# Two pipelined halves in one fixed order per step: attention over time, then attention over bands with feed-forward in the same step

## The chip, the cores and the metric

The kernel runs on one core of one Trainium2 chip. The metric is the device time of one execution in microseconds; most executions agree within 0.3%. The TensorE clock is granted by a throttle; the profile gives it as a share of full speed.

TensorE does the matmuls (PE in the profile, its weight loads PEld), VectorE is DVE, ScalarE is ACT, GpSimd is POOL. SBUF is working memory, PSUM the accumulator that matmuls write.

## The reference

One block of a model on x of shape 2 x 256 x 128 x 128 (batch, time T, bands F, channels C), all in fp32: three residual branches, each with a layer norm.

```python
xt = _ln(x, ln_t_w, ln_t_b).transpose(0, 2, 1, 3)
x = x + _mha(xt, ..., H_T, causal_mask).transpose(0, 2, 1, 3)   # attention over T, 4 heads of 32
xf = _ln(x, ln_f_w, ln_f_b)
x = x + _mha(xf, ..., H_F, band_mask)                           # attention over F, |i - j| <= 16
xn = _ln(x, ln_n_w, ln_n_b)
h = gelu(xn @ w1.T + b1)                                        # 128 -> 512
x = x + (h @ w2.T + b2)                                         # 512 -> 128
```

## The kernel before

Work is cut into groups of 512 rows (NT = 4 tiles of 128). The first half has 128 groups of attention over time and writes x1 to DRAM. The second half loads 16 time steps at a time, does band attention for four groups and then feed-forward for the same four. Program order is group after group; a scheduler may reorder each engine's queue.

```python
def attention_bands(self, src, dst, after):
    qT, kT, v = self.project(src, 1)          # norm, transpose xp -> xnT, qp, kp, vp
    sp = self.ps_s.tile([P, H, 512], F32, name="sp")
    ...                                       # 16 score matmuls
    p = self.pw.tile([P, H, NT * P], F32, name="pb", tag="p")
    for h in range(0, H, 2):
        e = nc.scalar.activation(p[:, h : h + 2], sp[:, h : h + 2], AF.Exp)
        ...                                   # two masks on POOL
    op = self.ps.tile([P, NT * P], F32, name="op", tag="ps")   # values
    sm = self.ps.tile([P, NT * P], F32, name="sm", tag="ps")   # row sums, by a matmul with ones
    ...
    self.add_attended(dst, op, sm, 1)         # divide on DVE, yp = oT @ wo, add

def feed_forward(self, cur, res, after):
    xnT = self.norm_transposed(lambda i: cur[:, i, :])
    for j in range(NI):
        hp = ps.tile([P, NT * P], F32, name="hp", tag="ps")    # one bank each, four rotate
        nc.tensor.matmul(hp, self.w1[:, j * P : (j + 1) * P], xnT, start=True, stop=True)
        e = nc.scalar.activation(hT[:, j, :], hp, AF.Gelu, bias=..., scale=1.0)
    zp = ps.tile([P, NT, P], F32, name="zp", tag="ps")
    ...

# PSUM, eight banks: four for the scores, four that rotate for everything else
self.ps_s = ctx.enter_context(tc.tile_pool(name="ps_s", bufs=1, space=PSUM))
self.ps = ctx.enter_context(tc.tile_pool(name="ps", bufs=4, space=PSUM))
```

## Time and profile before

| | before |
|---|---|
| time | 5907.1 us, median of 3 |
| TensorE busy / mean clock | 69% / 0.81 |
| first half | 128 groups of 17.2 us |
| second half | 128 groups of 28.7 us |
| PE busy and clock, 100 to 2200 us | 67%, 0.83 |
| PE busy and clock, 2300 to 5800 us | 72%, 0.79 |

The busy row counts an engine from start to end of its instructions. A TensorE busy share below 100% at a clock below 1 has two losses in it: time without a matmul, and matmuls that run at half rate. The prediction shows the lines.

### The profile page before, as it was taken

Reading aid. Unit: us, or ns where it says so; the run is one execution under the profiler, and the core shown is the slowest. Engines: PE = TensorE matmul, PEld = TensorE weight load, DVE = VectorE, ACT = ScalarE, POOL = GpSimd, SP = SyncE. Lnnn points to the kernel's source line nnn. Section 1 sums busy time; section 2 is a strip of 40 time slices with the busy share of each in tenths; the row PEclk is TensorE's granted clock in tenths of the full one; section 3 lists DMA queues with packets and bytes.
Section 4 is the critical chain, followed back from the end, with each engine's and each line's share of the span. In section 5 each row is a group of like instructions: output and inputs, shape, how many; then the busy total and the mean of one; then the engine's idle time right before and its main releaser. Section 6 shows DMA issues by size and latency. Waiting matters only on the chain. (4 is left out here: it accounts for less than half of the span.)

```text
span 5915.1 us, 79997 instructions
## 1 busy us (share of the span) xinstructions
PE 4105.8 (69%) x33318; PEld 2701.9 (46%) x33318; DVE 2042.5 (35%) x6314; ACT 1603.7 (27%) x1984; POOL 1805.4 (31%) x2086
## 2 busy tenths in 40 slices
PE   5666666666666666767677766767776776777677
PEld 3444444444444444445444444544444454444445
DVE  4333333333333323333333333333333333333332
ACT  2222222222222222223222222222222232222222
POOL 3222223222222222333333333333323333332332
PEclk9888888888888788778777887877787787788778
DMA  2111111111111110000000000000000000000000
GB/s 56 31 31 29 38 31 30 31 31 29 38 31 29 29 29 26 15 15 22 22 15 17 27 15 15 24 20 15 17 27 15 15 26 18 15 17 27 8 8 16
DMA packets 222867, 140.70 MB, mean 24 GB/s; under 512 B 7968, under 2 KB 205984, under 8 KB 222496
## 3 DMA queue, kind: packets, MB, share of 16 engines
q1 hardware_dynamic: 221248, 134.45, 8.2%
q8 instruction: 264, 4.33, 0.3%
q10 hardware_dynamic: 1248, 1.05, 0.1%
q14 instruction: 107, 0.88, 0.0%
HBM read 68.36 MB, written 67.11 MB: 23 GB/s over the span
## 5 line engine op out<-in xcount | busy, mean ns | idle before, releaser
L193 DVE TRANSPOSE_TENSOR_REDUCE st<-sm 128x16 f32<-128x512 f32 x256 | 183.3, 716 | 2402.1 <-PE sm L306 1473.5
L163 ACT COPY xnT<-xp 128x512 f32<-128x512 f32 x384 | 224.7, 585 | 2570.5 <-PE xp L161 2570.5
L294 POOL TENSOR_SCALAR_AFFINE_SELECT pb<-pb 128x1024 f32<-128x1024 f32 x512 | 541.0, 1091 | 1154.0 <-ACT pb L290 1154.0
L304 PE MATMUL op<-pb,v 128*32 128x128 f32 x4096 | 372.6, 409 | 611.7 <-POOL pb L294 611.7
L304 PEld LDWEIGHTS op<-pb,v 128*32 128x32 f32 x4096 | 216.4, 156 | 759.3 <-POOL pb L294 707.1
L216 PE MATMUL hp<-xnT,w1T_sb 128*128 128x512 f32 x1024 | 521.0, 651 | 39.0 <-ACT xnT L163 23.4
L224 PEld LDWEIGHTS zp<-w2T_sb,hT 128*128 128x128 f32 x4096 | 487.5, 192 | 61.5 <-issue 59.6
L224 PE MATMUL zp<-w2T_sb,hT 128*128 128x128 f32 x4096 | 499.0, 275 | 0.1
L153 POOL TENSOR_SCALAR rstd<-mv 128x4 f32<-128x4 f32 x384 | 92.0, 242 | 1311.3 <-DVE mv L151 1311.3
L217 ACT ACTIVATE hT<-hp,bias 128x512 f32<-128x512 f32 x512 | 351.9, 687 | 458.9 <-PE hp L216 458.4
L205 PE MATMUL yp<-f_woT_sb,oT 128*128 128x128 f32 x1024 | 234.2, 402 | 330.4 <-DVE oT L202 330.4
L252 POOL TENSOR_SCALAR_AFFINE_SELECT p<-p 128x512 f32<-128x512 f32 x512 | 313.2, 634 | 487.3 <-ACT p L249 487.2
L364 POOL TENSOR_TENSOR res<-x,rows_sb 128x512 f32<-128x512 f32 x128 | 162.1, 1266 | 976.6 <-DVE x L206 842.0
L205 PE MATMUL yp<-t_woT_sb,oT 128*128 128x128 f32 x1024 | 205.8, 363 | 341.4 <-DVE oT L202 341.4
L306 PE MATMUL sm<-pb,ones 128*32 128x512 f32 x1024 | 442.4, 962 | 0.0
L205 PEld LDWEIGHTS yp<-f_woT_sb,oT 128*128 128x128 f32 x1024 | 196.5, 286 | 512.9 <-DVE oT L202 512.9
L249 ACT ACTIVATE p<-sp 128x1536 f32<-128x1536 f32 x256 | 371.2, 1450 | 210.8 <-PE sp L245 200.2
L178 ACT ACTIVATE kT<-kp,bias 128x512 f32<-128x512 f32 x256 | 175.9, 687 | 868.4 <-PE kp L176 868.4
L154 POOL TENSOR_TENSOR rstd<-rstd,mhalf 128x4 f32<-128x4 f32 x384 | 403.5, 1053 | 16.2
L158 DVE TENSOR_SCALAR xh<-xb,mv,rstd 128x128 f32<-128x128 f32 x512 | 273.0, 596 | 326.0 <-PE xp L161 234.9
L205 PEld LDWEIGHTS yp<-t_woT_sb,oT 128*128 128x128 f32 x1024 | 172.8, 255 | 375.9 <-DVE oT L202 375.9
L270 PE MATMUL op<-p,v 128*32 128x256 f32 (+1 forms) x4096 | 281.9, 376 | 89.1 <-POOL p L252 89.1
(99 smaller groups left out, 6390.0 us busy)
## 6 DMA issues: line engine op xcount, KB each, us to landing
xt<-in_x SPq DMA_DIRECT2D x64, 512.0 KB, 5.4
x<-rd SPq DMA_DIRECT2D x256, 128.0 KB, 1.9
out<-res SPq DMA_DIRECT2D x128, 256.0 KB, 2.3
xb<-x SPq DMA_DIRECT2D x32, 0.5 KB, 6.2
w1T_sb<-in_w1T ACTq DMA_DIRECT2D x1, 256.0 KB, 4.1
w2T_sb<-in_w2T ACTq DMA_DIRECT2D x1, 256.0 KB, 4.5
t_wiT_sb<-in_t_wiT ACTq DMA_DIRECT2D x1, 192.0 KB, 2.6
f_wiT_sb<-in_f_wiT ACTq DMA_DIRECT2D x1, 192.0 KB, 4.0
```

What stands on the lines that cost most here:

```text
L154: nc.gpsimd.tensor_tensor(rstd, rstd, self.mhalf, ALU.pow)
L158: nc.vector.tensor_scalar(xh[:, i, :], src(i), mv[:, i, 0:1], rstd[:, i : i + 1], ALU.subtract, ALU.mult)
L205: nc.tensor.matmul(yp[:, i], oT[:, i * P : (i + 1) * P], self.wo[a], start=True, stop=True)
L216: nc.tensor.matmul(hp, self.w1[:, j * P : (j + 1) * P], xnT, start=True, stop=True)
L217: e = nc.scalar.activation(hT[:, j, :], hp, AF.Gelu, bias=self.bias[:, 4 + j : 5 + j], scale=1.0)
L224: nc.tensor.matmul(zp[:, i], hT[:, j, i * P : (i + 1) * P], self.w2[:, j, :], start=(j == 0), stop=(j == NI - 1),)
L249: e = nc.scalar.activation(p, sp[:, :, 0 : 3 * P], AF.Exp)
L252: nc.gpsimd.affine_select(out=d, in_=d, compare_op=ALU.is_ge, fill=0.0, base=0, pattern=[[0, H], [1, P]], channel_multiplier=-1,)
L270: nc.tensor.matmul(to[r, t0 + (2 - m) * P : t0 + 2 * P], v[:, 2 * s + n // 2, r] if left is None else left, p[:, h, n * P : (n + m) * P], ...
L294: nc.gpsimd.affine_select(out=d, in_=d, compare_op=ALU.is_ge, fill=0.0, base=BAND, pattern=[[0, 2 * NT], [s, P]], channel_multiplier=-s,)
L304: nc.tensor.matmul(op[r, t], v[:, i, r], p[:, h, t], start=True, stop=True)
L306: nc.tensor.matmul(sm[h * D : (h + 1) * D], self.ones, p[:, h], start=True, stop=True)
```

## The change

The intent is to keep TensorE fed. Each group's work is cut into phases; a loop issues, in every step, phases of neighbouring groups in one order on TensorE, DVE, ACT and POOL, and the scheduler may not change it. Band attention and feed-forward (two groups behind) share a step. PSUM is split anew: four banks for scores **or** hidden (one buffer), one each for op and sm, two that rotate for xp, qp, kp, vp, yp and zp.

```diff
+    def hidden(self, g):
+        nc, NI = self.nc, self.NI
+        hp = self.ps_s.tile([P, NI, 512], F32, name="hp", tag="s")
+        g.hT = self.work.tile([P, NI, NT * P], F32, name="hT", bufs=2)
+        for j in range(NI):
+            nc.tensor.matmul(
+                hp[:, j], self.w1[:, j * P : (j + 1) * P], g.xnT, start=True, stop=True
+            )
+            nc.scalar.activation(
+                g.hT[:, j], hp[:, j], AF.Gelu, bias=self.bias[:, 4 + j : 5 + j], scale=1.0
+            )
...
+    def pipeline(n, phases):
+        ...
+        for t in range(-before, n + behind):
+            for f, off in phases:
+                if 0 <= t + off < n:
+                    f(t + off)
...
-        self.ps = ctx.enter_context(tc.tile_pool(name="ps", bufs=4, space=PSUM))
+        self.ps_o = ctx.enter_context(tc.tile_pool(name="ps_o", bufs=1, space=PSUM))
+        self.ps = ctx.enter_context(tc.tile_pool(name="ps", bufs=2, space=PSUM))
+        ET = mybir.EngineType
+        ctx.enter_context(
+            tc.manual_schedule(engines={ET.PE, ET.DVE, ET.Activation, ET.Pool})
+        )
...                                            # first half: 14 phases; second half:
+        self.pipeline(len(hs), [
+            (load_b, 8),
+            (add_y_b, -1),
+            (lambda n: self.scores_bands(hs[n]), 0),
+            (lambda n: self.norm_turn(hs[n]), -2),          # xp, xnT of feed-forward
+            (lambda n: self.project_q(hs[n], 1), 1),
+            (lambda n: self.norm_apply(hs[n], lambda i: hs[n].x[:, i, :]), 2),
+            (lambda n: self.project_kv(hs[n], 1), 1),
+            (stats_b, 3),
+            (lambda n: self.hidden(hs[n]), -2),
+            (lambda n: self.values_bands(hs[n]), 0),
+            (begin_c, -1),
+            (lambda n: self.shrink(hs[n]), -2),             # zp
+            (lambda n: self.divide_sums(hs[n]), 0),
+            (lambda n: self.divide(hs[n]), 0),
+            (lambda n: self.norm_apply(hs[n], lambda i: hs[n].x2[:, i, :]), -1),
+            (lambda n: self.project_out(hs[n], 1), 0),      # yp
+            (lambda n: self.norm_turn(hs[n]), 2),           # xp, xnT of attention
+            (add_z, -2),
+        ])
```

## The prediction

> **What bounds the kernel now.** I read the busy row and the clock row of the page first, then the waits, then stretches and the timeline of each half.
>
> ```profile
> PE 4105.8 (69%) x33318; PEld 2701.9 (46%) x33318; DVE 2042.5 (35%) x6314; ACT 1603.7 (27%) x1984; POOL 1805.4 (31%) x2086
> ...
> PEclk9888888888888788778777887877787787788778
> ```
>
> No engine is near its limit: TensorE 69%, the others about a third, at a clock of about 0.8. TensorE is idle for 5915 - 4106 = 1809 us, and part of its 4106 us is slow. The waits say what the idleness is:
>
> ```profile
> ACT xnT L163 <- PE xp L161: 2570.5, 384, 16.8
> DVE st L193 <- PE sm L306: 1473.5, 128, 12.8
> ...
> PE yp L205 <- DVE oT L202: 671.8, 256, 3.9
> PE op L304 <- POOL pb L294: 611.7, 128, 5.8
> ```
>
> (engine and line, what it waited for: us in all, times, longest.) Every engine waits for another, in both directions. That is one group's chain run nearly serially: transpose, q/k/v, scores, exp, mask, values, divide, output projection. The two TensorE waits shown are 1283 us. The timeline of one band group (start, length) shows it:
>
> ```profile
> 4018.42 2.08 PE L172 MATMUL qp<-xnT,f_wiT_sb 128*128 128x512 f32 x2 [0.73 <-ACT xnT L163]
> ...
> 4023.17 1.17 PE L286 MATMUL sp<-qT,kT 32*128 32x128 f32 x32
> ...
> 4024.49 1.94 ACT L290 ACTIVATE pb<-sp 128x1024 f32<-128x1024 f32 x2 [0.57 <-PE sp L286]
> 4025.59 4.23 POOL L294 TENSOR_SCALAR_AFFINE_SELECT pb<-pb 128x1024 f32<-128x1024 f32 x4 [5.35 <-ACT pb L290]
> 4028.82 0.14 PEld L304 LDWEIGHTS op<-pb,v 128*32 128x32 f32 x4 [4.67 <-POOL pb L294]
> ...
> 4035.71 1.80 PE L205 MATMUL yp<-f_woT_sb,oT 128*128 128x128 f32 x8 [2.58 <-DVE oT L202]
> ```
>
> The stretches (length, then busy us of PE, PEld, DVE, ACT, POOL, clock, DMA share, GB/s) put a band group beside a run of feed-forward groups:
>
> ```profile
> 4017.00:4037.70 20.70, 12.91 (x98) 7.86 (x97) 6.02 (x19) 3.79 (x5) 6.73 (x7) 0.75 0.00 1
> 4048.40:4072.00 23.60, 23.07 (x136) 16.80 (x135) 9.81 (x16) 10.01 (x15) 5.79 (x2) 1.00 0.14 37
> ```
>
> The band group uses TensorE for 12.9 of 20.7 us at clock 0.75; feed-forward is dense (98%) at 1.00, some 7.5 us a group. The first half (time attention) runs from 30 to about 2230 us, 128 groups of 17.2 us; the second from about 2235 to 5910, 128 groups of 28.7 us, attention and feed-forward in turns of four.
>
> The clock is a cost of its own: kp takes 1.02 us in some places, 1.91 in others. Binning the trace into the 3.41 us windows at which its clock record changes, and taking TensorE's busy share in each: of 325 full-clock windows under 40% busy every one is followed by a half-clock window, of 352 over 60% none; a half-clock window is followed by a full one only when over 70% busy, mostly over 90%. So gaps cost twice.
>
> **What the Trainium skill says.** "TensorE: Matmul & The Clock Gate", Part 1, gives half rate after an idle window of about 3.4 us and full rate after a busy one; this trace agrees, sharpened by the counts above. The same part says that one or two busy cores never trip the peak-current limit, so I expect a dense single core to keep 1.00, as it does in the stretch shown. "PSUM — Partial Sum Buffer", Specifications, has 8 banks of 2 KiB: both kernels use all (before 4 for scores and 4 rotating; after 4 for scores or hidden, 1+1 for op and sm, 2 rotating). "ScalarE: Activation LUTs", What ACT_TABLE_LOAD costs, has 1283 ns a load plus a 1380 ns drain; the trace has the 1283, but a load starts 0.03 us after the copy before it, so I count no drain.
>
> **The change, part by part.** No matmul or elementwise work is removed (but for larger x2 adds being split: 32 of 4.53 us become 128 of about 1.27, off the path). What changes is that each engine's queue interleaves neighbouring groups, in one order.
>
> *TensorE work per step at full clock*, as time from a phase's first matmul to the next phase's in the full-clock parts of the trace: xp 0.44, qp 0.86, kp 0.86, vp 0.98, yp 1.00, time scores 0.87 and time values 1.31 per half, hp 3.44, zp 3.57. Band values had no full-clock instance: op 2.0 and sm 1.6 at half clock, so estimated 1.1 and 0.86. Band scores 1.0. Sums: time step 0.44+0.86+0.86+0.98+1.00+2x0.87+2x1.31 = 8.5 us; band plus feed-forward step 2x0.44+0.86+0.86+0.98+1.0+1.1+0.86+1.0+3.44+3.57 = 14.6 us. Floor 128 x 23.1 = 2957 us.
>
> *First half.* Other engines per step, from the durations of the groups view: DVE about 6.3 us, ACT 4.8 (two Exp of 1.45, two copies of 0.585, kT 0.69), POOL 5.1: all below 8.5. I walked one step through by hand with those durations and about 0.05 us a handover. Exp of half 0 (ends 2.4 us in) hides behind xp and the previous group's values (to 2.6); masks and divide hide behind the next group's projections. Left: vp waits some 0.15 us for its bank (qT on DVE). About 8.7; I take 9.0 for waits that I overlooked: 128 x 9.0 = 1152 us against 2200. Dense, so full clock.
>
> *Second half.* ACT per step: 2x0.585 + 0.69 + 0.585 + 2x1.02 + 4x0.69 + two table loads of 1.28 = 9.8 us. The loads rise from 64 (in the trace) to 252 (258 in the built order less 6 in the branch not taken): 188 x 1.28 = 241 us of ACT, not all hidden: the Exp load waits for the scores. The walk, 0 at the first score: scores end 1.17, load to 2.57, two Exp to 4.5, then the feed-forward xnT copy to 5.1. TensorE meanwhile does scores, xp and qp, to 2.3. Then the two rotating banks bind: one holds qp (freed by qT on DVE at 3.25), the other xp (freed by that copy at 5.1). In the built order kp takes the qp bank in 85 steps and the xp bank in 40 (its wait names DVE or ACT). In the 85, kp runs 3.3 to 4.2 and vp waits to 5.2: 2.0 us idle, step 16.6. In the 40, kp waits to 5.2: 2.9 us idle, step 17.5. From there hp, values, zp and yp run on (hT ready 11.1, zp begins 11.6; oT ready 13.2, yp begins 15.1; add_z ends 16.1, about when xp wants the bank). Mean 16.9 us.
>
> These gaps are where a 3.41 us window can be under half busy. I take a 30% chance in the 85 and 85% in the 40, each costing one half-clock window, 1.7 us of work lost: about 0.8 on average. Step 17.6: 128 x 17.6 = 2253 us against 3675.
>
> *Sum.* 30 (setup as before) + 1152 + 2253 + about 70 for filling and draining the two pipelines and the turn between them (estimate: eight partial steps) = **3505**, say 3500 us.
>
> **The rivals.**
> - *A new wait takes the place of the old.* Fixed order stalls every engine behind its head, and two rotating banks instead of four couple kp and vp to ACT and DVE. For: the 2 to 3 us above, and scores and hidden sharing one buffer. Against: ACT, DVE and POOL have 40% slack per step. If each step of the second half lost 3 us more: about 3900.
> - *The clock stays low.* If the second half locks into a half-clock window per step, or two: 19 to 20 us a step, 3700 to 3800. If the gaps never suffice: 16.9, about 3410.
> - *ACT becomes the bound through the table loads.* 9.8 of 17 us says no; with a 1.38 us drain per load 12.6, still no, though 1.4 us would land on the Exp chain: +180 us.
> - *DVE and POOL block one another.* In the trace four xh, 1.11 us elsewhere, took 5.47 us while POOL ran the 4.53 us x add. The longest POOL add is now 1.27 us, and both engines have slack. Mostly hidden.
> - *Transfers bind.* 59 GB/s in the first half instead of 31, at a DMA share of about a quarter, loads issued eight steps ahead: hidden.
> - *Gain hidden anyway.* TensorE's waits are on the path, since nothing else is busy; I see no way for it to stay near 5900.
>
> **Range and chances.** Low end: 8.7 and 16.6 us steps, 3240 + 100, about 3340, less a little if my phase times overlap: 3270. High end: locked half-clock windows plus something overlooked, 3850. Predicted 3500; faster is almost certain, since even a loss of 10 us a step leaves 4800.
>
> **What would show it right or wrong.** In the profile after: PE busy share about 85% or more; clock about 1.00 in the first half, 0.9 or more in the second; first half about 1150 us, second about 2250; yp waiting for oT and op for pb nearly gone; new TensorE waits at kp and vp, on ACT xnT and DVE qT, some 2 to 3 us a step; 252 table loads. Wrong if the first-half step exceeds 10 us (a wait that I missed in a dense order), if the second half's clock is below 0.85 (the gaps feed the throttle more than I gave), or if another wait (xp for add_z, zp for hT, sm for pb) tops the list.

## The result

The changed kernel takes 4280.65 us (median of 4 runs, 4280.25 to 4280.98) against 5909.43 us of the kernel before in the same rounds. Ratios in this document are the mean time of one kernel's fast runs over that of the other's of the same rounds, so not quite the ratio of the medians; here it is 0.7242 (0.723 to 0.7255). The experiments ran on three chips, in rounds in which the kernel before took 5908 to 5925 us (medians), so a difference of some 20 us between two rounds should not be read. The direction was right, but the time is 780 us above the 3500 us predicted and outside the range.

The page of the changed kernel, busy row and clock row:

```profile
PE 3599.9 (84%) x33318; PEld 2180.9 (51%) x33318; DVE 2147.6 (50%) x6314; ACT 1808.9 (42%) x2172; POOL 1834.9 (43%) x2182
...
PEclk9999999999999988888888888888888888888888
```

The clock row splits the run in two. The stretches of the changed kernel (length, then busy us of PE, PEld, DVE, ACT, POOL, the clock, DMA share, GB/s), one in each half:

```profile
300.00:1100.00 800.00, 800.00 (x10306) 537.50 (x10298) 535.49 (x1544) 397.47 (x429) 425.65 (x600) 1.00 0.22 59
1500.00:3300.00 1800.00, 1421.38 (x10563) 807.92 (x10563) 789.14 (x2343) 718.47 (x906) 705.47 (x753) 0.86 0.08 23
```

The first half is full: TensorE is busy all the time at full clock, and a step takes 9.34 us (0.3 us above the prediction). The second half is not: a step takes 23.90 us (mean of 90 steps) against 17.6 predicted; TensorE is idle for a fifth of it and the clock is 0.86. Nearly the whole miss lies there: over all its steps the mean is 23.5 us, and 128 x 5.9 = 760 of the 780 us. TensorE's waits in the changed kernel (line, waited for: us in all, times, longest):

```profile
PE hp L393 <- ACT hT L396: 428.3, 384, 1.8
PE kp L276 <- ACT xnT L264: 94.6, 39, 2.4
PE kp L276 <- DVE qT L271: 71.8, 85, 0.8
PE vp L283 <- ACT xnT L264: 39.1, 85, 0.7
```

The last three are the waits that the prediction had. The first it had not: 384 waits are three in each of 128 steps, at hp, the hidden matmuls, for hT, the result of Gelu. No hidden matmul reads hT. In the kernel before, no such wait stands beside this line (x count, busy us and mean ns, then the idle time before it and what ended it):

```profile
L216 PE MATMUL hp<-xnT,w1T_sb 128*128 128x512 f32 x1024 | 521.0, 651 | 39.0 <-ACT xnT L163 23.4 <-DVE res L228 15.6
```

The timeline of one step of the changed kernel (start, length, ...) shows how it comes:

```profile
3013.41 1.02 PE L393 MATMUL hp<-xnT,w1T_sb 128*128 128x512 f32 x2
...
3014.22 1.28 ACT L396 ACT_TABLE_LOAD   x1
3015.51 0.69 ACT L396 ACTIVATE hT<-hp,bias 128x512 f32<-128x512 f32 x1
...
3016.25 1.12 PE L393 MATMUL hp<-xnT,w1T_sb 128*128 128x512 f32 x2 [1.81 <-ACT hT L396]
...
3017.41 0.69 ACT L396 ACTIVATE hT<-hp,bias 128x512 f32<-128x512 f32 x1 [1.22 <-PE hp L393]
...
3018.16 2.07 PE L393 MATMUL hp<-xnT,w1T_sb 128*128 128x512 f32 x2 [0.78 <-ACT hT L396]
...
3020.27 0.69 ACT L396 ACTIVATE hT<-hp,bias 128x512 f32<-128x512 f32 x1 [2.16 <-PE hp L393]
3021.00 0.50 PEld L393 LDWEIGHTS hp<-xnT,w1T_sb 128*128 128x128 f32 x2 [2.35 <-ACT hT L396]
3021.01 2.08 PE L393 MATMUL hp<-xnT,w1T_sb 128*128 128x512 f32 x2 [0.78 <-ACT hT L396]
3023.01 0.20 PEld L378 LDWEIGHTS sm<-pb,ones 128*32 128x32 f32 x8 [1.50 <-issue]
```

Matmul, Gelu, matmul, Gelu, strictly in turn. Matmul j+1 writes bank j+1 of hp while Gelu j reads bank j; it starts 0.05 us after that Gelu's end all the same. The first Gelu also waits for its table load. From the first hp to sm it takes 9.6 us for work of 3.4. And from the third matmul on it is slow: 2.07 and 2.08 us where the first took 1.02. The clock has gone to half.

What the clock costs can be read in the same trace, since the first steps of the second half still have it in full. Two steps with the same waits (kp 0.84 us, hp 1.82, 0.78 and 0.78), one early and one later:

```profile
1306.10:1326.90 20.80, 16.13 (x145) 10.06 (x144) 10.41 (x32) 9.49 (x12) 9.37 (x10) 1.00 0.05 15
1573.80:1597.50 23.70, 19.03 (x145) 10.75 (x144) 10.45 (x32) 9.49 (x12) 9.37 (x10) 0.86 0.04 12
```

Of the steps with these waits, seven at full clock take 20.8 us each, 78 with half clock 23.7: 2.9 us a step are the clock. From 1489 us on its record repeats one pattern nearly to the end, 6.83 us at half and 17.07 at full, 23.9 us in all, which is the mean step. The steps have locked to the windows of 3.41 us in which the clock changes, seven to a step, two of them at half.

**Theory A.** The four banks of hp are one tile, and the order of its writes and reads is kept tile-wide: matmul j+1 must wait for the reader before it, whatever bank it touches. Since every engine's order is fixed, TensorE can do nothing else in the meantime. The gaps then bring the half clock, which costs time of its own.

**Rivals.** B: ACT's own work, the 252 table loads above all, sets the step. C: the clock stays low for another reason, and the waits matter little. D: the bank coupling at kp and vp (the waits in the prediction) is what feeds the half clock.

### The profile page after: what moved, and what is told of

Read it like the earlier page. It is cut to its first block, busy times and chain, and to the rows that moved or that the text cites. A ratio compares the mean times of both kernels' runs of the same rounds, so it can differ in the third digit from the quotient of the medians.

```text
span 4278.5 us, 79873 instructions
## 1 busy us (share of the span) xinstructions
PE 3599.9 (84%) x33318; PEld 2180.9 (51%) x33318; DVE 2147.6 (50%) x6314; ACT 1808.9 (42%) x2172; POOL 1834.9 (43%) x2182
## 4 chain that ended last, share of the span: by engine, by line
PE 75%; ACT 20%; issue 3%; DVE 1%; DMA 0%; POOL 0%; ACTq 0%; SPq 0%; DVEq 0%; POOLq 0%
PE hp L393 15%; PE zp L404 11%; PE vp L283 7%; ACT hT L396 6%; PE yp L310 6%; ACT pb L365 6%; PE sm L378 5%; PE sp L324 5%; PE sm L347 5%; PE op L347 4%; ACT L396 4%; PE kp L276 4%; PE sp L362 3%; PE xp L262 3%; PE qp L269 3%
## 5 line engine op out<-in xcount | busy, mean ns | idle before, releaser
L393 PE MATMUL hp<-xnT,w1T_sb 128*128 128x512 f32 x1024 | 775.4, 849 | 433.0 <-ACT hT L396 428.3
L393 PEld LDWEIGHTS hp<-xnT,w1T_sb 128*128 128x128 f32 x1024 | 192.1, 235 | 837.9 <-ACT hT L396 832.5
L271 DVE TENSOR_SCALAR qT<-qp,bias 128x512 f32<-128x512 f32 x256 | 192.2, 751 | 352.0 <-PE qp L269 352.0
L253 DVE TENSOR_SCALAR xh<-xb,mv,rstd 128x128 f32<-128x128 f32 x512 | 355.0, 755 | 1.5 <-POOL rstd L248 1.5
L276 PE MATMUL kp<-xnT,f_wiT_sb 128*128 128x512 f32 x256 | 146.5, 655 | 166.5 <-ACT xnT L264 94.6
L262 PE MATMUL xp<-ident,xh 128*128 128x128 f32 x1536 | 253.4, 288 | 16.2 <-DVE xh L253 16.2
L365 ACT ACTIVATE pb<-sp 128x1024 f32<-128x1024 f32 x256 | 248.1, 1021 | 3.1 <-PE sp L362 1.7
L324 PE MATMUL sp<-qT,kT 32*128 32x256 f32 (+1 forms) x4096 | 239.4, 347 | 1.2 <-ACT p L329 1.2
L378 PE MATMUL sm<-pb,ones 128*32 128x512 f32 x1024 | 235.8, 1005 | 3.1 <-POOL pb L368 3.1
L347 PE MATMUL sm<-p,ones 128*32 128x256 f32 (+1 forms) x4096 | 219.5, 332 | 0.0
```

Of the source, the lines that this page charges most:

```text
L253: self.nc.vector.tensor_scalar(g.xh[:, i, :], src(i), g.mv[:, i, 0:1], g.rstd[:, i : i + 1], ALU.subtract, ALU.mult,)
L262: nc.tensor.transpose(xp[:, i * P : (i + 1) * P], g.xh[:, i, :], self.ident)
L324: nc.tensor.matmul(sp[:, h, n * P : (n + m) * P], kT[r, k : k + P], qT[r, k : k + m * P], start=True, stop=True,)
L347: self.nc.tensor.matmul(to[r, t0 + (2 - m) * P : t0 + 2 * P], g.v[:, 2 * s + n // 2, r] if left is None else left, g.p[s][:, h, n * P : (n ...
L365: nc.scalar.activation(g.p[:, h : h + 2], sp[:, h : h + 2], AF.Exp)
L378: nc.tensor.matmul(g.sm[h * D : (h + 1) * D], self.ones, g.p[:, h], start=True, stop=True)
```

## The experiments

Each edit is to the changed kernel (4280.65 us), but for e9 (to e7) and e10 (to e1). All results were right except where said. Step and PE busy are of the second half (90 steps; the first half's step is 9.34 us in all but e8 and e9). Idle is the step less the busy share of it; e.g. for the changed kernel busy is 1421.38/1800 x 23.90 = 18.9 us.

| run | us | ratio to before | step us | PE busy us | idle us | clock |
|---|---|---|---|---|---|---|
| changed kernel | 4280.65 | 0.724 | 23.90 | 18.9 | 5.0 | 0.86 |
| matmuls first (e1) | 3476.73 | 0.589 | 17.20 | 15.3 | 1.9 | 1.00 |
| gaps filled (e2) | 3994.47 | 0.676 | 21.44 | 18.9, 2.6 of it dead | 2.6 | 0.98 |
| one table (e3, wrong) | 3715.14 | 0.629 | 19.16 | 15.9 | 3.3 | 1.00 |
| early copy (e4) | 3916.61 | 0.663 | 20.75 | 16.7 | 4.1 | 0.98 |
| first and early (e5) | 3341.34 | 0.565 | 16.22 | 15.7 | 0.5 | 1.00 |
| one-bank tiles (e6) | 3570.68 | 0.604 | 18.09 | 15.6 | 2.5 | 0.97 |
| pairs and early (e7) | 3323.85 | 0.562 | 16.12 | 16.0 | 0.1 | 1.00 |
| free order (e8) | 3936.24 | 0.665 | 19.49 | 17.2 | 2.3 | 0.94 |
| e7 in free order (e9) | 4082.26 | 0.689 | 20.86 | 18.9 | 2.0 | 0.95 |
| e1 with dead matmuls (e10) | 3759.31 | 0.635 | 19.49 | 18.1, 2.6 of it dead | 1.4 | 0.99 |

### e1: the four hidden matmuls, then the four Gelu

```diff
         for j in range(NI):
             nc.tensor.matmul(
                 hp[:, j], self.w1[:, j * P : (j + 1) * P], g.xnT, start=True, stop=True
             )
+        for j in range(NI):
             nc.scalar.activation(
```

> Edit: the four hidden matmuls of a group are issued first, then the four Gelu (in the changed kernel they alternate, and each hidden matmul waits for the Gelu before it although it writes another bank of the same four-bank tile). Theory A (that tile-wide wait, with the half clock that its gaps bring, is the 6 us a step that the prediction lacked): the second half's step falls from 23.7 us to about 18.5, the hidden phase from 9.6 us to about 3.5, PE's wait for hT before hp vanishes and a smaller one (about 1 us) comes before zp; in all about 3670 us (3500 to 3800). Rival B (the table loads and ACT's own work set the step): ACT has the same work, so at least 4100 us. Rival C (the clock stays low whatever the gaps at hp): the wait goes but the clock stays at 0.9, about 4000 us.

Measured: 3476.73 us (3461.72 to 3486.93, with mean clocks of 0.995 to 0.986; the trace is of the fastest). The stretch of the second half of e1, to be held against the second line of the changed kernel's:

```profile
1500.00:3300.00 1800.00, 1606.23 (x14685) 1095.83 (x14683) 1092.61 (x3245) 963.18 (x1256) 981.47 (x1046) 1.00 0.11 31
```

One added loop header gives 804 us. The timeline of e1:

```profile
2613.47 3.60 PE L393 MATMUL hp<-xnT,w1T_sb 128*128 128x512 f32 x8
...
2614.28 1.28 ACT L397 ACT_TABLE_LOAD   x1
...
2617.00 1.06 PE L378 MATMUL sm<-pb,ones 128*32 128x512 f32 x8
2617.11 2.42 ACT L397 ACTIVATE hT<-hp,bias 128x512 f32<-128x512 f32 x4 [1.55 <-PE hp L393]
...
2618.87 3.88 PE L405 MATMUL zp<-w2T_sb,hT 128*128 128x128 f32 x32
```

The hidden phase takes 3.5 us. Gelu now waits for all four matmuls (the tile-wide order once more: it starts 0.1 us after sm does, not after the first hp), but sm and op run beside it, and zp hardly waits. Theory A holds, and B falls: ACT has the same work and loads. The time lies below the expected range (3500 to 3800), since I had still counted half-clock windows and a wait of 1 us before zp: of the windows few are left (six half-clock spells of one window each, and one at the very end), of the wait almost nothing (1.9 us in all). With the false wait gone the kernel runs within 1% of the 3500 us predicted for the change; how far that is luck is told below.

### e2: more work in the gaps

```diff
+        dead = self.ps_o.tile([P, NT * P], F32, name="dead", tag="op")
         for j in range(NI):
             ...                                  # matmul hp[:, j], then Gelu, as before
+            if j < NI - 1:
+                nc.tensor.matmul(
+                    dead, self.w1[:, j * P : (j + 1) * P], g.xnT, start=True, stop=True
+                )
```

> Edit: in the changed kernel, after each of the first three hidden matmuls one dead matmul of the same size (0.86 us at full clock) into a spare bank, nothing reads it; the result stays right. It adds 3 x 0.86 us of TensorE work a step and takes no wait away. Theory A (the gaps cost twice, by waiting and by the half clock): the gaps are filled, the clock stays full, hidden 9.6 to about 7.2 us and the sums after it 1.7 to 0.9, the step about 20.4 us, in all about 3870 us, faster with more work. Rival (the half clock is no matter, the waits alone are): 4280 us or up to 330 us more.

Measured: 3994.47 us, **286 us faster with 384 more matmuls** of 0.86 us. The stretch of e2:

```profile
1500.00:3300.00 1800.00, 1585.40 (x12260) 967.07 (x12260) 876.65 (x2604) 800.10 (x1008) 788.62 (x840) 0.98 0.09 26
```

The Gelu waits are all still there in the program, but mostly covered (119 of the 384 are left at hp, 109 us in all). What is won is the clock, 0.86 to 0.98: the kernel's own matmuls fall from 18.9 to 18.9 - 2.6 = 16.3 us a step. So the half clock costs at least 2.6 us a step by itself (about 330 us), which fits the 2.9 read above, and rival C, that it is apart from the gaps, falls. The gain is less than expected (3870 us): the gap before the second hp is only part filled, and the kp wait still brings half-clock windows: 30 of the 32 half-clock spells of the second half come at a kp wait of 2.4 us.

### e3: Gelu replaced by Exp, no table loads (wrong result)

```diff
-                g.hT[:, j], hp[:, j], AF.Gelu, bias=...
+                g.hT[:, j], hp[:, j], AF.Exp, bias=...
```

> Edit: Gelu replaced by Exp, wrong result on purpose; the same durations on ACT but no table loads (252 less 1 of 1.28 us). Theory A: the Gelu load delays the first hidden activation by about 1 us and the Exp load the projections by about 0.5 to 1.3 us, so 1.5 to 2.3 us a step: 3990 to 4090 us. Rival B (the loads are the main loss): 3.9 us a step or more, below 3800 us.

Measured: 3715.14 us (relative error 0.48, as intended). This **missed my expectation** and fell where I had put rival B. The waits say why it is not B. TensorE's waits at hp, kp and vp fall from 634 to 416 us, that is 1.7 us a step, inside the 1.5 to 2.3 expected. The hp wait in e3:

```profile
PE hp L393 <- ACT hT L396: 298.7, 384, 0.8
```

All 384 are there, but the longest is 0.8 us instead of 1.8: the load no longer stands in the first one. The other 3.0 us a step are TensorE's busy time, 18.9 to 15.9, at a clock of 1.00. With 1 us off the largest gap at hp, and the Exp load's share off the gaps at kp and vp (206 us become 117), the half clock all but stays away: two spells in the second half, both at its end. Which of the two loads matters more this run does not show. The loads do matter, then, but through the clock and beside the tile-wide wait: e1, with all 252 of them, is faster than this run without. I had left the clock out of this expectation.

### e4: the feed-forward copy ahead of the Exp

```diff
+            (lambda n: self.norm_turn(hs[n]), -2),
             (lambda n: self.scores_bands(hs[n]), 0),
-            (lambda n: self.norm_turn(hs[n]), -2),
```

> Edit: in the second half the transposes and the copy xnT of the feed-forward group are issued ahead of the band scores and their Exp, instead of after, so that the two rotating banks are not held behind the Exp. Theory A: the waits of kp and vp on xnT go (1.3 us a step in 85 steps, 2.4 us in 40), the hidden waits stay: step about 22 us, in all about 4075 us (3950 to 4150). Rival D (the bank coupling of kp and vp is what feeds the half clock): clock in the second half up to 1.0 and below 3850 us.

Measured: 3916.61 us, below the range expected. The stretch of e4 and its wait at hp:

```profile
1500.00:3300.00 1800.00, 1446.70 (x12168) 897.08 (x12164) 830.06 (x2691) 824.39 (x1043) 808.03 (x870) 0.98 0.09 26
PE hp L393 <- ACT hT L396: 442.4, 384, 1.9
```

The waits of kp and vp are gone, those of hp are not; idle falls by 1.0 us a step, and busy by 2.2 with the clock at 0.98. So kp's gap takes part in what pulls the clock down, beside hp's: rival D is right in part, though its mark (below 3850 us) was not reached. The two gaps lie within some 6 us of one another (3010 to 3016 us in the step shown). Taking out the one at kp (here), the ones at hp (e1), or a piece of each (e3) mostly cures the clock.

### e5: e1 and e4 together

> Edit: both of the edits that helped, together: the four hidden matmuls ahead of the four Gelu, and the feed-forward transposes and copy ahead of the band scores. If what was left in the first (231 us of TensorE waits at kp and vp) is the copy behind the Exp, it goes: step from 17.2 to about 15.6 us (hp may now wait some 0.4 us for the Exp to give the shared buffer back), in all about 3260 us (3200 to 3350). Rival: the waits move to hp or zp one for one and it stays near 3450 us.

Measured: 3341.34 us, inside the range. What is left are a wait of hp for the Exp to give the shared buffer back, 0.37 us a step, and one of 0.2 us at xp.

### e6: one-bank tiles, order of issue unchanged

```diff
-        hp = self.ps_s.tile([P, NI, 512], F32, name="hp", tag="s")
         for j in range(NI):
+            hp = self.ps_s.tile([P, 512], F32, name=f"hp{j}", tag="s")   # pool of four one-bank tiles
             nc.tensor.matmul(
-                hp[:, j], self.w1[:, ...
+                hp, self.w1[:, ...
```

The scores become four one-bank tiles too, with an Exp each; the pool is one of the second half's own.

> Edit: hidden matmuls and Gelu alternate as in the changed kernel, but each of the four hidden tiles (and of the four score tiles) is a one-bank tile of its own, from a pool of four. Theory A (the wait is there because the four banks are one tile): the wait of hp for hT goes with the order of issue unchanged, about 3480 us (3400 to 3560), as with the matmuls first. Rival (alternating itself is to blame, each Gelu handing back to TensorE): about 4280 us.

Measured: 3570.68 us. Matmul and Gelu alternate in the program as in the changed kernel, and the wait at hp is gone, as the timeline of e6 shows:

```profile
2612.93 3.60 PE L394 MATMUL hp<-xnT,w1T_sb 128*128 128x512 f32 x8
```

So it is the tile, not the alternation: theory A. The 90 us more than the 3480 expected (11 above the range) have a name in the waits of e6:

```profile
PE kp L276 <- ACT xnT L264: 311.9, 125, 2.8
```

In this build kp takes the bank of xp in all 125 steps, 2.5 us each, and 37 of the 39 half-clock spells of the second half come at this wait. Which of the two rotating banks a tile gets is decided when the program is built, and shifts from build to build: kp waits in the xp bank in 40 steps of the changed kernel, 62 of e1, 125 here.

### e7: two-bank tiles and the early copy, the best version

```diff
-        sp = self.ps_s.tile([P, H, 512], F32, name="sp", tag="s")
+        sp = [self.ps_s.tile([P, 2, 512], F32, name=f"sp{k}", tag="s") for k in range(2)]
...
-        hp = self.ps_s.tile([P, NI, 512], F32, name="hp", tag="s")
+        for j0 in range(0, NI, 2):
+            hp = self.ps_s.tile([P, 2, 512], F32, name=f"hp{j0}", tag="s")
+            ...                                  # matmuls j0, j0 + 1, then Gelu j0, j0 + 1
```

> Edit: the shared four-bank buffer of the second half as two two-bank tiles (scores of heads 0-1 and 2-3; hidden 0-1 and 2-3, two matmuls then two Gelu each), and the early copy. The first hidden pair waits for the first Exp only and Gelu starts after two matmuls: no wait over 0.2 us left in the second half but zp's, step about 15.2 us, in all about 3220 us (3150 to 3320). Rival: the step is held by something else (masks on POOL, the divide on DVE), 3260 us or more, no better than both edits on the one buffer.

Measured: 3323.85 us, 4 us above the range, ratio 0.5618 to before, 0.776 to the change by the medians (3323.85/4280.65). The page of e7:

```profile
PE 3260.3 (98%) x33318; PEld 2193.5 (66%) x33318; DVE 2153.2 (65%) x6314; ACT 1763.4 (53%) x2172; POOL 1826.1 (55%) x2182
...
PEclk9999999999999999999999999999999999999999
```

Both halves are now bound by TensorE at full clock. The expected step of 15.2 us was too low, 16.1 measured: TensorE is busy for 16.0 of it (15.3 in e1). Part of that are the two transposes, now one after the other, 1.4 us to the next start instead of 1.1 in e1: the weights of the second wait 0.37 us for x on DVE in the timeline of e7, a price of the early copy (1.45 us in e5). Part are the sums and values, which take 2.4 us to the next start instead of 1.9: in the timeline of e7 the weight load of the last sums waits 0.42 us for a mask on POOL, with other matmuls drawn out around it. So e7 is only 17 us better than e5, and the rival, masks on POOL, has a share in it.

### e8 and e9: without the fixed order

```diff
-        ctx.enter_context(
-            tc.manual_schedule(engines={ET.PE, ET.DVE, ET.Activation, ET.Pool})
-        )
```

> Edit: the changed kernel without the fixed order: phases and buffers as they are, but the scheduler may reorder each engine's queue (in the built order it puts sums, values and later matmuls between the hidden ones). If the wait at hp hurts since the fixed order leaves nothing to run in it, the order found fills part of it: 3700 to 4100 us. If the fixed order is worth more than that (first half above all, 9.34 us a step now), 4280 us or more.

> Edit: the best version so far (two-bank tiles and early copy, 3324 us) without the fixed order. Theory: the fixed order is worth its 1.03 us a step in the first half (10.37 against 9.34 us, as measured without it) and some 0.5 to 2 us in the second, once no wait is left in it: 3520 to 3710 us. Rival (the fixed order has no worth of its own, the offsets between the phases do it all): within 2% of 3324 us.

The changed kernel in free order (e8) takes 3936.24 us, faster than in its fixed order. In its second half the scheduler puts values, zp and yp between the hidden matmuls, so the false wait is filled: 19.5 us a step. In the first half it is slower, 10.7 us a step on average (the 10.37 in e9's expectation is the median, which I took for the mean) against 9.3, as a stretch of e8 shows:

```profile
300.00:1100.00 800.00, 759.93 (x8884) 490.25 (x8886) 429.64 (x1325) 344.29 (x370) 362.05 (x518) 0.99 0.18 50
```

The best version in free order (e9) takes 4082.26 us, 758 us more than e7, and 370 more than the top of what I expected. The first half ends 187 us later than in e7 (at 1417 us instead of 1230), the second accounts for the other 570, 4.7 us a step in the table: busy 18.9 instead of 16.0 at clock 0.95, idle 2.0 instead of 0.1, with kp and qp waiting for xnT (161 and 83 us in all). So a fixed order is worth much where it has no wait in it, and costs where it has one. Which displacement in e9 costs most was not tried and stays open.

### e10: control, dead matmuls where there is no gap

The edit is that of e2, in e1: a dead matmul between each two hidden matmuls.

> Control: the same three dead matmuls a step as in the filled gaps, but in the kernel with the four hidden matmuls first (3477 us), where there is no gap at hp for them to fill. Theory A (dead work costs its full time where TensorE is dense; it paid only by keeping the clock up): 3 x 0.86 x 128 = 330 us more, 3800 us (3740 to 3850). Rival (dead matmuls in this place help or cost nothing for another reason, the order at hp for one): below 3650 us.

Measured: 3759.31 us, 283 us more than e1, where the work alone is 330 us. Dead work costs nearly its price where TensorE is dense, so what it won in e2 was not due to its place. The 47 us short of the price fit with the bank choice: kp takes the xp bank 18 times here, 62 in e1, and the waits of kp and vp come to 182 us in all instead of 231.

## Why the prediction was right or wrong

- **What bounds the kernel: right.** Serial chains and a clock pulled down by gaps. With the gaps out (e7) TensorE is the bound at 98% and full clock.
- **First half: right, the sum a little small.** 9.34 us a step for 8.5 plus waits, 1195 us for 1152. The phases were mis-sized, not the waits: xp takes 0.59 us to the next start for 0.44, qp 0.96 for 0.86, kp 1.01 for 0.86 (the wait for vp's bank included), vp 1.09 for 0.98, yp 1.09 for 1.00, the values of a half 1.43 for 1.31. I had taken them from other neighbours; here each stands beside a phase that splits the array otherwise (see the last section).
- **Second half: the step that failed** is "From there hp, values, zp and yp run on (hT ready 11.1, zp begins 11.6; ...)". It took hp as dense, 3.44 us, once the shared buffer was free. It takes 9.6: three false waits, the first with the table load in it (3.3 us of TensorE wait a step in the trace), and the half clock. In a step of the first kind (kp in the qp bank) this is 20.8 us at full clock against 16.7 in e1, so 4.1 us for what the waits at hp cost, and 2.9 more for the half clock, against 0.8 allowed. The prediction read the built order for the waits of kp, not for those of hp. The hidden tiles had been four separate ones before the change, so the wait is new. e1 and e6 remove it in two ways, and the wait at hp and nearly all of the loss go with it.
- **The gaps at kp and vp: right.** With hp out of the way (e1) the median step is 16.69 us with kp in the qp bank and 17.55 in the xp bank; predicted 16.6 and 17.5. That is partly luck: the phases were 0.7 us too short in sum (e1's busy 15.3 against 14.6), and the waits of kp and vp came out 0.7 us shorter than walked, at 1.3 us (0.84 and 0.46) in the one kind.
- **The clock: mechanism right, place and size wrong.** I gave it 0.8 us a step from the kp and vp gaps. Alone they bring little: in e1 six spells of one window in 125 steps, in e6, with kp in the xp bank each time, 37. With the hp gaps every step has two windows at half, 2.9 us a step. (A recount of the windows in the prediction gives 308 to 325 under 40%, by how the bins are laid, and some 460 over 60% where it has 352; what they are followed by stands. Its 16.9 + 0.8 is 17.7, not 17.6.)
- **The rivals.** "A new wait takes the place of the old" and "the clock stays low" were both named, at 3900 and 3700 to 3800, but as alternatives. They came together, since the one feeds the other, and the sum lay outside the range. The lock of the clock to the step was named there too, at 19 to 20 us, on top of a step without the hp waits. Among the waits that were to be looked for as signs of being wrong, hp for hT was not. The table loads landed on the path in one place that I had not seen, the first Gelu. Transfers stayed hidden (DMA share 0.22 in the first half).
- **The range** was too narrow for this reason: the losses that feed the throttle do not add up one by one.

## What to carry to other kernels

In a pipeline of fixed order, look for waits of each instruction on one that it doesn't read from: a multi-bank PSUM tile that one engine fills while another empties it is ordered as a whole, so give each bank (or pair) its own tile, or issue all writes before the first read. Gaps in TensorE of more than about half of a 3.4 us window cost twice here (the counts are in the last section), so judge a wait together with its neighbours; here e4 and e3, which took 1.0 and 1.7 us of waiting out of a step, won 2.8 and 4.4 us a step. The step can also lock to the clock's windows, as in the changed kernel, and then every step pays for two of them at half. Fix the order only after the waits are out: here the fixed order lost 344 us with the false wait in it and won 758 without.

## What the Trainium skill lacked or had wrong

- "TensorE: Matmul & The Clock Gate", Part 1, speaks of an idle window and a busy one, and gives no share of busy time that makes a window the one or the other. The changed kernel's trace, binned in the 3.41 us windows of its clock record, shows it for this case: a full-clock window with TensorE under 40% busy was followed by half clock in all of 102 cases, at 40 to 50% in 18 of 62, at 50% or more in none of 841. Back to full clock it went only after windows over 90% busy (119 of 119); half-clock windows at 60 to 80% stayed at half clock in all 118 cases. So a window need not be wholly idle to lose the clock. In the kernel before, 45 of 240 windows of 50 to 60% were also followed by half clock, and 60 of 258 half-clock windows of 70 to 90% by full clock, so neither edge is sharp.
- "ScalarE: Activation LUTs", What ACT_TABLE_LOAD costs, adds a 1380 ns drain to the 1283 ns load. The load took 1.28 us in every trace here, and no drain: in the changed kernel's timeline it starts 0.03 us after the copy before it, and Gelu 0.01 us after the load.
- "TensorEngine Tiling (Array Packing)", Key Properties, says that a change of tiling mode drains TensorE, but no size. The traces are in keeping with it: xp, on the whole array, takes 0.59 us to the next start before sums in tiles of 32 columns, 0.49 before qp on the whole array in the second half, and 0.44 between feed-forward phases on the whole array in the kernel before. That would be some 0.1 to 0.15 us a change (an estimate from these three; that the drain is the cause was not tested).
- No page has it that a PSUM tile of several banks is ordered as one between a writer and a reader of different banks. It is a property of how the program is built, not of the chip, and together with the half clock it cost 804 us of 4281.
